# A branch moved to the kernel's end, layer 0's update around the last gathered rows, and layer 1's end bank by bank

## The chip, the core and the metric

The kernel runs on one core of a Trainium2 chip. A core has several engines that each work through a queue of their own: TensorE (PE, with its weight loads listed as PEld), VectorE (DVE), ScalarE (ACT), GpSimd (POOL) and SyncE (SP), which here only starts transfers. They wait for each other through semaphores. Sixteen DMA engines move the data. The metric is the device time of one execution in microseconds; lower is better.

## The reference

Four graph layers run one after another on the same 2708 nodes with 128 features each (`x`) and one 2708 by 2708 matrix `adj`, about 2.4% of which is not zero. After each layer stands a residual normalization.

```python
x = layernorm(x + layer0(x, adj))   # likewise layers 1, 2, 3

def layer0(x, adj):                 # a message for every edge
    s, d = x @ msg_w[:, :D].T, x @ msg_w[:, D:].T
    messages = gelu(s[:, None, :] + d[None, :, :] + msg_b)
    aggregated = einsum('ijd,ij->id', messages, adj)
    new = concatenate([x, aggregated], -1) @ upd_w.T + upd_b
    h = gelu(new) + x
    return normalize(h) * ln_w + ln_b

def layer1(x, adj):                 # gates for every pair
    m = x @ W_msg + b_msg
    gates = sigmoid((m @ W_q) @ (m @ W_k).T / sqrt(128) + gate_bias)
    aggregated = (gates * adj * adj) @ m
    h = relu(concatenate([x, aggregated], 1) @ W_upd + b_upd)
    return normalize(h) * gamma + beta
```

Layers 2 (hyperbolic attention) and 3 (two graph convolutions with swish) keep their code in this change; only where they stand in the program changes.

## The kernel before

The 2708 rows lie in 22 tiles of up to 128 partitions (`NT`; the last has 20 rows). Work that ends in a bank of PSUM (512 floats per partition) goes by `groups()`: five groups of four tiles, then tile 20 alone, then tile 21 with its 20 rows. The normalizations go by `runs()`, two halves of eleven tiles.

**Layer 0** never forms all pairs. It takes 22 row tiles of 125 rows against 22 blocks of 124 columns, picks up to five edges per row and block with one-hot products on PE (L716, L721), applies Gelu on ACT (L760), weighs on DVE (L747) and adds up on PE (L732). The rows' remaining, "far" edges, up to 16, are gathered one by one: `start_far` (SP) lays the row's own part from a table in DRAM, `s_tab`, into a buffer `far`, eight indirect transfers on POOL add the other end's part to it (L680), ACT applies Gelu (L686), DVE sums up with the edges' weights (`far_sum`, L692 and L694), and `turn` and `close` (PE L700 to L703, ACT L706) put the row tile's result into `aggT`. All of this is ordered by hand: every row tile yields steps with the number of the block at which each is due (`when`), and the loop over 484 blocks runs the steps that are due. Steps that are due beyond the last block remain; for the last row tile these are the second Gelu, eight far sums, `turn` and `close`.

Behind the loop a counter is made: `bad_n` (L777 to L785) is the number of rows with more far edges than there is room for, or with values that aren't finite. Then the remaining steps run. Then `new`, x's half of the update, which an earlier stage has stored in the table `u_tab`, is loaded (L791), `bad_n` is read into a register on every engine, and a branch (L793, L794) leads to a second way that goes through all pairs. With these inputs it is not taken. Then the update: POOL makes `xb`, x plus `ln_b` (L846); per group PE multiplies `aggT` with `upd_a` (L851), DVE adds `new` (L852), ACT applies Gelu (L853), DVE adds x (L854) and takes the statistics (`bn_stats`, L173). `resnorm` then normalizes by halves: a chain of some fifteen small DVE operations with one square root on ACT (the table of functions is loaded for it, L121), the normalization of the eleven tiles, two of three on DVE (L194) and the third on ACT (L192), times `ln_w` (L201), plus `xb` (L202), statistics again, and a second normalization into x. From the branch on, the order on each engine is not written by hand; the framework's scheduler lays groups and halves into each other.

**Layer 1** begins by multiplying the two gate weights into one (L880 to L885), turns x on PE (xT, L892, L893), forms the messages twice, turned (`mT`, L895, L896) and by rows (`mrow`, `sums` at L231 and L233), and `qT` (L898, L899); POOL makes `xb` (L901). Then 22 rows of tiles follow: six products into two buffers of PSUM (`lg`, L922), the sigmoid on ACT (L923) into a gate buffer `w` (two of them), two multiplications by the row of adj on DVE (L925, L926), and six products with `mrow` that add up in six banks of PSUM over all 22 rows (`acc`, L928). Then six copies to `aggT` (L930), the update (`sums` of x's and of the aggregate's half, Relu at L942), and `resnorm`. Small values of layer 2's weights are made beside this (`Weights2`: vectors by POOL's queue, L264, and a chain from L270 on).

SP's queue is in program order: the far rows, `new`, three of layer 1's rows of adj (`at`, L911), four of layer 2's (L1122), then each further row as buffers come free; at the end the `out` transfers.

Of the kernel before, what the change touches and what calls it, by code (L numbers as in the profile page):

```python
# [11 lines left out]
F32 = mybir.dt.float32  # L12
# [26 lines left out]
def gnn_stack(ctx: ExitStack, tc: tile.TileContext, t, out: bass.AP):  # L39
# [13 lines left out]

    def weight(name, k0=0):
        w = const.tile([P, D], F32, name=f"w_{name}_{k0}")
        nc.sync.dma_start(out=w, in_=t[name][k0:k0 + P, :])
        return w

    def column(name):
        c = const.tile([P, 1], F32, name=f"col_{name}")  # L60
        nc.sync.dma_start(out=c, in_=t[name].rearrange("(p o) -> p o", o=1))
        return c

    def across(name):
# [8 lines left out]
    nc.vector.memset(x[:, NT - 1, :], 0.0)  # L73
    if NFULL:
        nc.sync.dma_start(out=x[:, :NFULL, :], in_=t["x"][:NFULL * P, :].rearrange("(n p) d -> p n d", p=P))
    if NFULL < NT:
        nc.sync.dma_start(out=x[:rows[-1], NT - 1, :], in_=t["x"][NFULL * P:, :])
# [14 lines left out]
    class Values:  # L92
# [5 lines left out]
        def new(self, like=None):  # L98
            self.n += 1
            shape = [P, NT] if like is None else list(like.shape)  # L100
            return self.pool.tile(shape, F32, name=f"{self.tag}{self.n}")

# [93 lines left out]
    def resnorm(h, xb, g, st, V, sq=None):  # L196

        st2 = V.pool.tile([P, NT, 6], F32, name=f"{V.tag}_st2")
        for a, b in runs():
            normalize(h, h, st, a, b, V)  # L200
            nc.vector.tensor_tensor(h[:, a:b, :], h[:, a:b, :], over_tiles(g, b - a), op=ALU.mult)  # L201
            nc.vector.tensor_tensor(x[:, a:b, :], xb[:, a:b, :], h[:, a:b, :], op=ALU.add)  # L202
            moments(st2, x, a, b)
        for a, b in runs():
            normalize(x, x, st2, a, b, V, sq)
# [119 lines left out]
    with ExitStack() as l0:  # L325
# [6 lines left out]
        bad_n = wp.tile([1, 1], mybir.dt.int32, name="bad_n")  # L332
# [4 lines left out]
        with ExitStack() as msg:  # L337
# [167 lines left out]
            class Rows:  # L505
# [125 lines left out]
                def past(self, m):  # L631
                    if m == 0:
                        self.o = op_.tile([P, NB, JB], F32, name="o")
# [105 lines left out]

            LAG = 3  # L740
            assert NC == 5 and NB % 2 == 0
            R = [Rows(i) for i in range(LT)]
            steps = sorted(((g, n, step) for n, (g, step) in enumerate(x for v in [preparation(), *(v.when() for v in R)] for x in v)),
                           key=lambda x: x[:2])
            with tc.manual_schedule():
# [27 lines left out]

                most = vp.tile([P, 1], F32, name="most")
# [12 lines left out]
                for _, _, step in steps:  # L787
                    step()

        new = l0.enter_context(tc.tile_pool(name="l0x", bufs=1, reuse_waits="tile")).tile([P, NT, D], F32, name="new")  # L790
        nc.sync.dma_start(out=new, in_=u_tab.rearrange("(n p) d -> p n d", p=P))  # L791

        n_bad = nc.values_load(bad_n[0:1, 0:1])  # L793
        with tc.If(n_bad > 0), ExitStack() as msg:  # L794
            mp = msg.enter_context(tc.tile_pool(name="all", bufs=1))
            ap_ = msg.enter_context(tc.tile_pool(name="adjrows", bufs=2))
            gp = msg.enter_context(tc.tile_pool(name="gelu", bufs=3))
            psum = msg.enter_context(tc.tile_pool(name="ps_l0", bufs=2, space=PSUM))
            pbc = msg.enter_context(tc.tile_pool(name="ps_bc", bufs=2, space=PSUM))
# [3 lines left out]
            sel = mp.tile([3 * RG, RG], BF16, name="sel")  # L803
            nc.vector.tensor_add(sel, ident[:3 * RG, 0:RG], ident[:3 * RG, RG:2 * RG])
            nc.vector.tensor_add(sel, sel, ident[:3 * RG, 2 * RG:3 * RG])

            xT = mp.tile([P, N], F32, name="xT")
            sT = mp.tile([P, N], F32, name="sT")
            dT = mp.tile([P, N], F32, name="dT")
            transposed(xT, x, psum)  # L810
            linear_T(sT, msg_s, xT, psum, bias=msg_b)
            linear_T(dT, msg_d, xT, psum)

            HALF_N = -(-N // 2)
            halves = spans(0, N, HALF_N)
            part = mp.tile([P, N, len(halves)], F32, name="part")
            for g0 in range(0, N, RG):
                r0 = min(g0, N - RG)
                a = ap_.tile([3 * RG, N], F32, name="a")
                for k in range(3):  # L820
                    nc.sync.dma_start(out=a[k * RG:(k + 1) * RG, :], in_=adj[r0:r0 + RG, :])
                s = ap_.tile([3 * RG, N], BF16, name="s")
                nc.gpsimd.tensor_copy(s, a)
                for n in (2 * RG, RG):
                    nc.gpsimd.tensor_tensor(a[:n, :], a[:n, :], s[:n, :], op=ALU.subtract)
                    nc.gpsimd.tensor_copy(s[:n, :], a[:n, :])
                for i in range(g0, min(g0 + RG, N)):
                    one = sel[:, i - r0:i - r0 + 1].to_broadcast([3 * RG, P])
                    g = gp.tile([P, N], F32, name="g")
                    nc.scalar.activation(g, dT, AF.Gelu, bias=sT[:, i:i + 1])  # L830
# [124 lines left out]
    with ExitStack() as l2:  # L955
# [27 lines left out]
        with ExitStack() as pre:  # L983
# [9 lines left out]
            for k in range(2):  # L993
                nc.gpsimd.memset(prod[k], 1.0)
# [527 lines left out]
```

## Time and profile before

The median of three executions is 2005.69 us (2005.01 to 2007.13). The execution that the profiler took had 2005.42 us, of which 2003.7 are its span, first to last instruction; 1.7 us lie around it.

| stage | from, us | to, us |
|---|---|---|
| layer 0, preparation and block loop | 0 | 894 |
| layer 0, last far rows, branch | 894 | 914 |
| layer 0, update and normalizations | 914 | 954 |
| layer 1, ahead of its row loop | 954 | 988 |
| layer 1, row loop | 988 | 1214 |
| layer 1, update and normalizations | 1214 | 1257 |
| layer 2 | 1257 | 1765 |
| layer 3 | 1765 | 2004 |

Over the whole span PE is busy for 1675.0 us (84%), DVE for 1517.8 (76%), ACT for 1105.9 (55%) and POOL for 666.0 (33%). The mean clock granted to PE is 0.918 of full speed.

A line of the timeline has the start in us, the duration in us, the engine, the line of the kernel, the operation, what it writes and reads with shapes, and how many lie in the group; in brackets, how long the engine stood idle before it, and what it waited for. "q" behind an engine's name is its instruction queue. In the table of windows "PEclk" is the share of full clock that PE was granted, and the last two columns are the DMA engines' mean share and their throughput.

### The profile page before, as it was taken

The numbers are of one execution on the slowest core, as the hardware profiler recorded it, in microseconds if no ns is written. First come the engines' busy times: TensorE is split into PE (matmuls) and PEld (weight loads), VectorE is DVE, ScalarE is ACT, GpSimd is POOL, SyncE is SP. The second block draws the span as 40 slices with busy tenths as digits, with TensorE's granted clock in tenths as the row PEclk, the third lists the DMA queues.
The fourth block names the chain that finished last, engine by engine and source line by source line (L and its number), as shares of the span: only waits on it lengthen the run. The fifth ranks groups of instructions, "written<-read, shape, count | busy, mean of one in ns | idle before, by whom it ended". The sixth has DMA issues, their size and how long they took to land. (4 is left out here: it accounts for less than half of the span.)

```text
span 2003.7 us, 36396 instructions
## 1 busy us (share of the span) xinstructions
PE 1675.0 (84%) x14037; PEld 959.1 (48%) x14037; DVE 1517.8 (76%) x3507; ACT 1105.9 (55%) x1510; POOL 666.0 (33%) x417
## 2 busy tenths in 40 slices
PE   5799999999999999871899994689999974079996
PEld 5566666666666666651444433423222322034543
DVE  5899999999999999857556567889999997820105
ACT  3567667666666676642333331599998993300103
POOL 2467767757767667461100000012000350000000
PEclk8899999999999999995899996779998987579998
DMA  7666666666667666343133310022222215135230
GB/s 178 155 139 131 133 136 140 126 136 148 124 133 148 130 129 139 73 85 143 36 135 136 142 60 0 1 87 87 75 80 94 80 42 245 46 115 187 107 127 28
DMA packets 218358, 222.25 MB, mean 111 GB/s; under 512 B 28372, under 2 KB 204474, under 8 KB 211714
## 3 DMA queue, kind: packets, MB, share of 16 engines
q1 hardware_dynamic: 167038, 195.95, 32.2%
q0 software_dynamic: 51136, 23.88, 10.3%
q8 instruction: 112, 1.84, 0.4%
q14 instruction: 72, 0.59, 0.1%
HBM read 211.94 MB, written 7.83 MB: 110 GB/s over the span
## 5 line engine op out<-in xcount | busy, mean ns | idle before, releaser
L680 POOL DMA_INDIRECT far<-d_tab,ix x352 | 563.0, 1599 | 257.5 <-DVE W L747 110.7
L760 ACT ACTIVATE g<-sl 128x768 f32<-128x768 f32 x484 | 393.0, 812 | 255.9 <-PE sl L721 199.1
L716 PE MATMUL sl<-dA,S 124*128 124x153 f16 x4840 | 408.0, 231 | 10.1 <-DVE W L747 7.7
L716 PEld LDWEIGHTS <-S 124*128 124x128 f16 x4840 | 330.4, 98 | 79.7 <-issue 67.9
L732 PE MATMUL acc<-g,W 128*32 128x128 f32 x4840 | 205.5, 277 | 0.7 <-DVE ones L777 0.7
L1125 POOL TENSOR_TENSOR at<-at,off 128x128 f32<-128x128 f32 (+1 forms) x22 | 68.1, 3113 | 338.1 <-DMA at<-in_adjT 320.4
L1441 PE MATMUL acc<-held,x 128*128 128x512 f32 (+1 forms) x240 | 99.6, 563 | 84.0 <-DVE x L194 84.0
L732 PEld LDWEIGHTS acc<-g,W 128*32 128x32 f32 x4840 | 140.6, 109 | 58.9 <-issue 54.7
L721 PE MATMUL sl<-s,same 50*128 50x384 f16 x968 | 161.9, 308 | 0.0
L233 DVE TENSOR_TENSOR g<-ps,row_L_gnn_b 128x512 f32<-128x512 f32 (+2 forms) x14 | 7.9, 572 | 197.1 <-PE ps L231 197.0
L923 ACT ACTIVATE w<-lg,row_L_gnn_gate_bias 128x512 f32<-128x512 f32 (+1 forms) x132 | 80.7, 634 | 137.8 <-PE lg L922 74.3
L1181 PE MATMUL accV<-m,X 128*128 128x512 f32 (+4 forms) x264 | 128.4, 628 | 33.6 <-DVE m L1171 29.2
L747 DVE TENSOR_TENSOR W<-sl,own 128x150 f32<-128x150 f32 x484 | 143.0, 299 | 14.6 <-ACT g L760 14.1
L1133 PE MATMUL ps<-XT 128*128 128x512 f32 (+4 forms) x264 | 143.2, 626 | 3.1 <-ACT m L1138 2.8
L676 DVE FIND_INDEX8 ix<-v,o 128x8 uint32<-128x2728 f32 x44 | 131.7, 2993 | 0.0
L607 DVE TENSOR_SCALAR S<-rk 124x1000 f16<-124x1000 bf16 (+1 forms) x330 | 129.4, 418 | 0.0
L922 PE MATMUL lg<-qT,mT 128*128 128x512 f32 (+2 forms) x264 | 115.5, 567 | 13.5 <-ACT w L923 9.9
L925 DVE TENSOR_TENSOR w<-w,at 128x2708 f32<-128x2708 f32 (+1 forms) x22 | 65.4, 2974 | 79.3 <-ACT w L923 79.3
L694 DVE SCALAR_TENSOR_TENSOR extra<-far,v,extra 128x128 f32<-128x128 f32 x330 | 114.4, 347 | 12.3 <-ACT far L686 6.0
L1441 PE MATMUL acc<-at,x 128*128 128x512 f32 (+3 forms) x288 | 116.7, 552 | 0.0
L638 DVE SCALAR_TENSOR_TENSOR o<-ps,ar 128x496 f32<-128x496 f32 x132 | 82.4, 624 | 38.3 <-issue 22.6
L1400 ACT COPY nT<-acc 128x512 f32<-128x512 f32 (+1 forms) x12 | 6.4, 530 | 186.7 <-PE acc L1441 186.7
(310 smaller groups left out, 2687.1 us busy)
## 6 DMA issues: line engine op xcount, KB each, us to landing
at<-in_adjT SPq DMA_DIRECT2D x40, 1354.0 KB
ar<-in_adj SPq DMA_DIRECT2D x105, 248.0 KB
far<-s_tab SPq DMA_DIRECT2D x44, 512.0 KB
at<-in_adjT SPq DMA_DIRECT2D x42, 448.0 KB
at<-in_adjT SPq DMA_DIRECT2D x21, 704.0 KB
at<-in_adjT SPq DMA_DIRECT2D x21, 650.0 KB
held<-in_adjT SPq DMA_DIRECT2D x10, 1354.0 KB
at<-in_adjT SPq DMA_DIRECT2D x21, 280.0 KB
```

The lines of the kernel that those rows point to most:

```text
L607: nc.vector.tensor_scalar(self.S[h][:, :n, :, k * RG:(k + 1) * RG], self.rk[h][:, :n, :LR].rearrange("p b (c i) -> p b c i", c=NC), EDGE + ...
L676: nc.vector.max_index(ix, self.v[:, n * 8:n * 8 + 8], self.o.rearrange("p b j -> p (b j)"))
L680: nc.gpsimd.indirect_dma_start(out=self.far[n][:, k, :], out_offset=None, in_=d_tab[:, :], in_offset=bass.IndirectOffsetOnAxis(ap=self.ix[ ...
L716: nc.tensor.matmul(group[c], self.S[h][:, n, c, :], dA[q][:, b, c, :], start=c % 3 == 0 and q == 0, stop=False)
L721: nc.tensor.matmul(out, same[p], self.s3[p, :e - a, :], start=False, stop=True)
L732: nc.tensor.matmul(self.acc[q:q + 32, k, :], W[:, c, :], g[:, c, :], start=b == 0 and k == 0, stop=ends)
L747: nc.vector.tensor_tensor(W[:, :, :RG].rearrange("p (k c) i -> p k c i", k=2), columns_of(sl, D, DA), own[:, None, None, :].to_broadcast([ ...
L760: nc.scalar.activation(g.rearrange("p (k c) d -> p k c d", k=2), columns_of(sl, 0, D), AF.Gelu, scale=1.0 / D_SCALE)
L922: nc.tensor.matmul(lg[:r, :b - a], mT[:, j * P:j * P + r], qT[:, a:b], start=True, stop=True)
L1133: nc.tensor.matmul(ps, XT[:, self.js], XT[:, c], start=True, stop=False)
L1181: nc.tensor.matmul(accV[:, a:b], X[:self.r, self.j, :], self.m[:, a:b], start=first, stop=last)
L1441: nc.tensor.matmul(acc[k], src[:rows[j], j, :], at[:rows[j], a:b], start=j == order[0], stop=j == order[-1])
```

## The change

It has three parts.

The branch: everything from layer 1 on becomes a function, `layers_1_to_3`. It runs once, and only then is `bad_n` read and the branch taken or not; inside of it x is loaded anew, layer 0 is done through all pairs, and layers 1 to 3 are done again. The loads of weights are cached, so that the second pass finds the first one's.

Layer 0's update: a class `Update` loads `new` during the block loop (due at block 469 of 484) into a buffer of the pool of rows `o`, and its groups are written by hand around the last row tile's remaining steps: the five groups that don't need the last row tile come first, with the last Gelu after the second and the eight far sums after the third. Then `turn` and `close`, the first half's normalization, the two last groups, and the rest. x plus `ln_b` is made in place on POOL, group by group. The counter `bad_n` comes last. Statistics and small values lie in two buffers `g` of the block loop (`Values.within`).

Layer 1: the products of x with `W_msg` and with x's half of `W_upd` become one, 256 wide, into `both` (two tiles per bank, one addition of the joint bias). There are four gate buffers instead of two; the accumulator is six tiles. The last three rows' products are held back and done bank by bank by hand: three products, the copy to `aggT` (on ACT instead of DVE), and the update of the bank before, which adds only the aggregate's half; the first half's normalization stands after the fourth bank. Ahead of the row loop, the stage takes all eight banks of PSUM.

```diff
+    class Resnorm:
...
+        def add(self, a, b):
+            h = self.h
+            normalize(h, h, self.st, a, b, self.V)
+            nc.vector.tensor_tensor(h[:, a:b, :], h[:, a:b, :], over_tiles(self.g, b - a), op=ALU.mult)
+            nc.vector.tensor_tensor(x[:, a:b, :], self.xb[:, a:b, :], h[:, a:b, :], op=ALU.add)
+            moments(self.st2, x, a, b)
+
+        def end(self, a, b):
+            normalize(x, x, self.st2, a, b, self.V, self.sq)
...
+            class Update:
+                def when(self):
+                    yield (LT - 1) * NB + 7, self.load
+
+                def load(self):
+                    o = op_.tile([P, max(NB * JB, NT * D)], F32, name="o")
+                    self.new = o[:, :NT * D].rearrange("p (n d) -> p n d", d=D)
+                    nc.sync.dma_start(out=self.new, in_=u_tab.rearrange("(n p) d -> p n d", p=P))
...
+                def sums(self, n):
+                    a, b, r = groups()[n]
+                    g, ps = self.new[:r, a:b, :], sl_all[n % 3][:r, n // 3 % 2, :].rearrange("p (i d) -> p i d", d=D)
+                    for i in range(a, b):
+                        nc.tensor.matmul(ps[:, i - a, :], aggT[:, i * P:i * P + r], upd_a, start=True, stop=True)
+                    nc.vector.tensor_tensor(g, g, ps[:, :b - a, :], op=ALU.add)
+                    nc.scalar.activation(g, g, AF.Gelu)
+
+                def rows(self, n):
+                    a, b, r = groups()[n]
+                    g = self.new[:r, a:b, :]
+                    nc.vector.tensor_tensor(g, g, x[:r, a:b, :], op=ALU.add)
+                    moments(self.st, self.new, a, b)
+                    nc.gpsimd.tensor_tensor(x[:r, a:b, :], x[:r, a:b, :], over_tiles(ln_b, b - a, r), op=ALU.add)
...
+                U.open()
+                for n in range(ahead):
+                    U.sums(n)
+                    if n > 0:
+                        U.rows(n - 1)
+                    if n == 1:
+                        last_gelu()
+                    if n == 2:
+                        for step in far_sums:
+                            step()
+                for step in last_turn:
+                    step()
+                U.rows(ahead - 1)
+                early, late = runs()
+                U.norm.add(*early)
+                for n in range(ahead, G):
+                    U.sums(n)
+                for n in range(ahead, G):
+                    U.rows(n)
+                U.norm.add(*late)
+                U.norm.end(*early)
+                U.norm.end(*late)
...
-                for _, _, step in steps:
-                    step()
-
-        new = l0.enter_context(tc.tile_pool(name="l0x", bufs=1, reuse_waits="tile")).tile([P, NT, D], F32, name="new")
-        nc.sync.dma_start(out=new, in_=u_tab.rearrange("(n p) d -> p n d", p=P))
-        n_bad = nc.values_load(bad_n[0:1, 0:1])
-        with tc.If(n_bad > 0), ExitStack() as msg:
...
+            both = wp.tile([P, NT, 2 * D], F32, name="both")
+            mrow, h = both[:, :, :D], both[:, :, D:]
...
-                sums(mrow[:r, a:b, :], a, b, r, [(xT, w_msg)], psum, msg_br)
+                    for i in range(a, b, 2):
+                        m = min(i + 2, b)
+                        ps = psum.tile([P, 2, 2 * D], F32, name="ps_w")
+                        for k in range(i, m):
+                            nc.tensor.matmul(ps[:r, k - i, :], xT[:, k * P:k * P + r], w_both, start=True, stop=True)
+                        nc.vector.tensor_tensor(both[:r, i:m, :], ps[:r, :m - i, :], over_tiles(b_both, m - i, r),
+                                                op=ALU.add)
...
-            gp = att.enter_context(tc.tile_pool(name="gates", bufs=2))
+                LAST = 3
+                gp = att.enter_context(tc.tile_pool(name="gates", bufs=LAST + 1))
...
+                def update(k):
+                    per = BANK // D
+                    for a, b, r in groups():
+                        if k * per <= a < (k + 1) * per:
+                            ps = plog.tile([P, BANK], F32, name="lg")[:r].rearrange("p (i d) -> p i d", d=D)
+                            for i in range(a, b):
+                                nc.tensor.matmul(ps[:, i - a, :], aggT[:, i * P:i * P + r], upd_a, start=True, stop=True)
+                            g = h[:r, a:b, :]
+                            nc.vector.tensor_tensor(g, g, ps[:, :b - a, :], op=ALU.add)
+                            nc.scalar.activation(g, g, AF.Relu)
+                            moments(st, h, a, b)
...
+                    if j < NT - LAST:
+                        for k in range(len(banks)):
+                            add_up(j, k, w)
+                    else:
+                        kept_w.append((j, w))
+                with tc.manual_schedule():
+                    early, late = runs()
+                    for k, (a, b) in enumerate(banks):
+                        for j, w in kept_w:
+                            add_up(j, k, w)
+                        nc.scalar.copy(aggT[:, a:b], acc[k])
+                        if k > 0:
+                            update(k - 1)
+                        if (k - 1) * BANK < early[1] * P <= k * BANK:
+                            norm.add(*early)
+                    update(len(banks) - 1)
+                    norm.add(*late)
+                    norm.end(*early)
+                    norm.end(*late)
...
+    with ExitStack() as top:
+        layers_1_to_3(top)
+
+    n_bad = nc.values_load(bad_n[0:1, 0:1])
+    with tc.If(n_bad > 0), ExitStack() as top:
+        load_x()
+        all_pairs()
+        layers_1_to_3(top)
```

## The prediction, made before the changed kernel ran

> **What bounds the kernel now.** I read the two stretches that the change rewrites, from layer 0's last row tile to layer 1's start (894 to 988 us) and layer 1's loop end to layer 2 (1200 to 1264), first as busy time by stage (columns: window, its length, busy us and instructions of PE, PEld, DVE, ACT, POOL, then granted clock, DMA share, GB/s).
>
> ```profile
> 894.00:908.00 14.00, 2.27 (x12) 1.64 (x8) 3.86 (x14) 1.94 (x6) 0.22 (x1) 0.63 0.43 113
> 908.00:914.00 6.00, 0.47 (x3) 0.76 (x4) 0.00 (x0) 0.00 (x0) 3.25 (x1) 0.50 0.37 117
> 914.00:954.00 40.00, 7.61 (x45) 6.80 (x44) 35.27 (x146) 11.50 (x26) 3.02 (x2) 0.59 0.39 160
> 954.00:970.00 16.00, 11.53 (x30) 6.88 (x31) 3.77 (x13) 4.21 (x7) 7.64 (x4) 0.63 0.16 13
> 970.00:988.00 18.00, 17.46 (x81) 10.65 (x81) 8.46 (x22) 8.03 (x17) 0.00 (x0) 1.00 0.00 1
> 988.00:1200.00 212.00, 200.14 (x495) 83.43 (x493) 124.00 (x44) 77.14 (x127) 0.00 (x0) 1.00 0.33 119
> ```
>
> For 20 us (894 to 914) nothing is busy for more than 4 us; then DVE is the bound (35 of 40), then PE at half clock, then PE at full clock, which holds the whole row loop. The timeline says what the first 20 us wait for, and how the loop ends:
>
> ```profile
> 892.13 0.71 SPq L791 DMA_DIRECT2D new<-u_tab  x1
> 901.37 1.06 ACT L686 ACTIVATE far<-far 128x1024 f32<-128x1024 f32 x1 [6.52 <-issue]
> 902.46 3.06 DVE L694 SCALAR_TENSOR_TENSOR extra<-far,v,extra 128x128 f32<-128x128 f32 x8 [6.02 <-ACT far L686]
> 907.50 0.26 ACT L706 COPY aggT<-ps 128x125 f32<-128x125 f32 x1 [5.08 <-PE ps L703]
> 913.53 7.39 PE L851 MATMUL ps<-w_L_upd_wT,aggT 128*128 128x128 f32 x44 [6.06 <-issue]
> 915.49 0.69 DVE L852 TENSOR_TENSOR new<-new,ps 128x512 f32<-128x512 f32 x1 [9.97 <-PE ps L851]
> ...
> 1200.52 4.81 PE L928 MATMUL acc<-w,mrow 128*128 128x512 f32 x12 [1.40 <-DVE w L926]
> 1206.40 7.51 PE L928 MATMUL acc<-w,mrow 20*128 20x512 f32 x12 [1.07 <-DVE w L926]
> 1213.94 3.30 DVE L930 COPY aggT<-acc 128x512 f32<-128x512 f32 x6 [7.60 <-PE acc L928]
> 1217.22 0.17 DVE L938 MEMSET h<- 128x128 f32 x1
> ```
>
> The last gather was issued by 894.2, yet its Gelu starts at 901.4: the u_tab load, issued at 892.1, fills the DMA engines meanwhile (share 1.04 and 1.02 in 896 to 900, 0.31 just before). After close (907.8) the branch L794 holds every engine until 910.7 and the first usable product until 913.5. At the loop's end the two last products and six copies run in series, 1200.5 to 1217.2.
>
> **The Trainium skill.** "TensorE: Matmul & The Clock Gate", Part 1, has the clock double after about 3.4 us of sustained work and fall after an idle window. Layer 1's tail agrees (restart 1217.4, full 1221.8), its start doesn't: restart 954.4, full at 969.6, with a gap at 963 to 966. "SBUF — State Buffer", Who interferes with whom, has a DVE operation with two SBUF inputs contend with a GpSimd one that reads SBUF; the trace agrees: L1125 on POOL takes 0.44 alone and 2.8 in the mean beside layer 2's vector work. "ScalarE: Activation LUTs", What ACT_TABLE_LOAD costs, gives 1283 ns plus a drain of 1380; the trace shows 1.28 and no drain.
>
> **Part 1, layer 0's update.** Removed: the load's collision, the branch in the middle, and the wait of the update for the last row tile; groups 0 to 4 are done while its far rows land. Added or moved onto DVE's path: nothing but order. On DVE from 895.3 (PE's first four products, 0.9 after the last weigh): per group the add .61 and, a group later, +x .56 with bn_stats .87, so 1.43. s0 .61, s1 .61, r0 1.43, s2 .61, r1 1.43 gives 900.0; the far rows should be there by then, so the far sums' 3.06 give 903.1; s3, r2, s4, r3, r4 (.61+1.43+.61+1.43+1.43) 908.6. add(early): the small-operation chain 2.65 (what the same chain takes at layer 3's end, 1977.9 to 1980.6, where order is also by hand), table load 1.28 exposed, normalize 2.16, ×ln_w 1.55, +x 1.55, bn_stats 2.15, .3 of gaps: 920.2. Groups 5 and 6: 1.8, 922.0. add(late), its table load hidden: 10.1, 932.1. end(early) 4.8, end(late) 4.6: 941.5. POOL's x+=ln_b, now in seven pieces beside two-input vector work (before, one of 6.12), costs 0 to 3; I take .8: x done at 942.3, where before it was 953.5. Then the bad_n count (895.1 to 896.5 before, hidden) stands ahead of layer 1 with w_q's transposes: 1.56 exposed. Layer 1's x transposes start at 945.4 against 954.8: −9.4. SP's order: the u_tab load now stands behind one far<-s_tab and ahead of the second, at about 868; that one, issued at 854.6 before, lands about 880.5 where its gathers want it at 879.7. 0 to 2 us, and hidden, since DVE reaches the far sums only at 900.0.
>
> **Part 2, layer 1's start.** Before, 954.8 to the first gate product at 988.3: 33.5. After: x's half of the update rides in 256-wide products, +.2 per tile of 22 on PE. The gap of 963 to 966 is DVE's L270, waiting until 965.0 for y_vecs, whose DMAs POOL issues only after xb (953.9 to 960.0); now POOL's xb begins when x is done, 3.1 ahead of PE's transposes, and at most 1 us of the gap is left. With the clock full 5 us after the start, as in layer 1's tail, qT is done 29.5 after, 974.9. PSUM is full now (four names by two buffers), so row 0's logits follow instead of lying between: 5.3, plus sigmoid's table load 1.28 and .5 of latency: 982.0. So −6.3 in all; 3.1 of the 9.4 go back. If PE stays at half clock as before, less: bounds −2 to −11.
>
> **Part 3, layer 1's loop.** Before, 988.3 to the last gates at 1206.4: 218.1. PE is full (200 of 212): 24 product records 9.48 and 12 logits pairs 10.94 per two rows. After, rows 19 to 21's products but one bank stand behind row 21's logits: .83 of a row's 4.74, −3.9. Four gate buffers let logits run ahead where PE waited for DVE (2.5) or ACT (9.9 in all): 0 to −4, I take −2. DVE is busy 124 of 212, but its last three rows then come in series, +.6. Last gates at 1194.8, −11.6.
>
> **Part 4, layer 1's tail.** Before, 1206.4 to layer 2's first scalar chain, 1263.3: 57.0. Now, per bank, three products at .86 and the update's .9 at .21 to .25 each, cold at first after some 5 us of waiting; ACT's copy .55; the moments of group 2 at +15.8, add(early) 10 after that (26), groups 3 to 6 at add .69, Relu .63, bn_stats .87 in series, 2.2 for the full two and .94 for the small two (32.4), add(late) 9.8, end(early) 6.5 with layer 2's memset and xsq, end(late) 5.9: +54.4, and 5.3 on to layer 2 (before, 6.1 from 1257.3; the late half's copies alone stand behind x now): 59.7. So +2.8: the pieces removed (6.6 of products and 3.3 of copies in series, half of the update's products) are paid back by DVE's hand-written order, which waits for ACT where the order of before filled the holes. Bounds −3 to +6.
>
> **Part 5, the branch at the end.** Its middle cost (907.8 to 913.5, 5.8) is in part 1. At the end each engine loads bad_n, compares and joins; L794's rows say from branch to join 5.1 on SP, 4.3 POOL, 2.9 DVE, 3.8 PE, 2.6 ACT.
>
> ```profile
> L794 SPq COMPARE_BRANCH  x1: 54/54/54, 897.0 to 897.0; - x1
> L794 PEldq COMPARE_BRANCH  x1: 3766/3766/3766, 906.2 to 906.2; - x1
> L794 ACTq COMPARE_BRANCH  x1: 50/50/50, 908.0 to 908.0; - x1
> ```
>
> SP issues its last out transfer at 2000.3 and would join about 2006; the span ends at 2003.7 for the transfers' sake. So +3, bounds +.5 to +6. SP's queue: layer 2's first at loads, issued at 914 before, now stand behind layer 1's 22 and wait for its buffers, to about 1240; four of 704 KB take some 16 us, wanted at about 1285: hidden, and up to +5 if not. Layers 2 and 3: 0.
>
> **Sum.** Layer 1 begins 9.4 earlier; its start gives 3.1 back (−6.3), its loop takes 5.3 (−11.6), its tail gives 2.8 back: −8.8 at layer 2. The branch at the end, +3: −5.8 on the profiled 2005.42, which stands .27 under the median of 2005.69. Forecast 1999.5 (1999.6 rounded); its own range is 1994.5 to 2002, from parts 3 and 5 alone at their ends.
>
> **Rivals.**
> R1, more gain: PE is warm within the first 5 us and row 0 follows closely (−4 more in part 2), the four buffers give their whole 4 (−2 more), and the branch hides behind the out transfers (+.5 for +3): −14.3, 1991. For: each removed wait is plain in the trace. Against: three parts have to come out at their good ends, and chains ordered by hand leave holes on DVE.
> R2, no change: POOL's additions take the 3 us (+2.2), the end costs 6 (+3): −.6, 2004.8; the late far rows or the tail at its worst give about the same. For: L1125's nineteen microseconds for its longest show how far POOL can fall behind DVE. Against: all of x+=ln_b is wanted only from 909 on, long after its issue.
> R3, slower, one mechanism: PE stays at half clock through layer 1's start, because the many small products keep waiting for ACT's and DVE's copies out of PSUM. The start holds 23 us of work counted at full clock (17.5 in 970 to 988, half of the 11.5 before) and now 4.4 more (.2 × 22); I have 2.5 of it doubled. With 12 more doubled: −5.8+12, 2011.6. It decides once more than 10 us (5.8 and the bound of 4) run at half clock beyond what I have. For: before, the clock was low through the first 15 us. Against: that stretch had its gap of 3 us, which goes.
>
> **How the numbers follow.** Forecast .47, R1 .23, R2 .20, R3 .10. A measurement of this kernel can't tell .2%, 4 us, from no change. Faster (under 2001.7): R1 and nearly all of the forecast's cases, .68. Same: most of R2, .21. Slower: R3 and a rest of R2, .11. The range takes in R1 with 2 us of its own spread and R2 with as much, and leaves R3 out: 1989 to 2007.
>
> **What would show it.** Part 1: x's last normalization at 942, no idle of 6 us on DVE ahead of the far sums. Part 2: first gate product near 982, clock 1.0 by 952. Part 3: last gates at 1195. Part 4: 57 to 60 us from there to layer 2. Part 5: last engine joins 3 us after the transfers. Wrong if the late far rows reach DVE's path, if layer 2's first rows wait for their at loads, or if the clock stays low.

## The result, and the profile after

The changed kernel takes 2010.91 us (median of 20 executions, 2004.5 to 2015.22) where the kernel before takes 2006.59 (median of 20, 2004.9 to 2008.41). The ratio is 1.0023, with a 95% interval of 1.0017 to 1.0029: slower by 0.2%, 4.3 us, where 5.8 us of gain were forecast. It also varies more: its executions lie 10.7 us apart, those of before 3.5.

The profiled execution took 2013.94 us, 3.0 above its kernel's median; its span is 2012.2, 8.5 more than before. The loop over layer 0's blocks, which the change doesn't touch, began its last weighing Gelu 2.8 us later in it (894.9 against 892.1; in the other runs of this study that point lies between 891.7 and 895.9). So the stages are compared from that point on. A gate product is DVE's product of a row's gates with its row of adj; the table has the start of the first and the end of the last, the "last gates". Layer 2's scalar chain is the run of small operations that DVE begins there. All values are us after the last weighing Gelu:

| until | before | after | forecast gain | measured gain |
|---|---|---|---|---|
| x of layer 0 is done | 61.4 | 51.9 | 11.2 | 9.5 |
| first gate product of layer 1 | 96.2 | 95.4 | 6.3 | 0.8 |
| last gate product's end | 314.2 | 304.8 | 11.6 | 9.4 |
| layer 2's scalar chain | 371.2 | 370.7 | 8.8 | 0.5 |
| DVE's last instruction | 1107.9 | 1108.4 | 8.8 | −0.5 |
| the span's end | 1111.6 | 1117.3 | 5.8 | −5.7 |

Every stage's gain comes and is given back in the stage after it. Layer 0's update gains 9.5, layer 1's start loses 8.7 of them; the row loop gains 8.6, the tail loses 8.9; the end loses 5.2. The table of windows of the changed kernel (columns as before):

```profile
894.00:914.00 20.00, 10.37 (x101) 8.39 (x98) 15.74 (x45) 5.79 (x12) 9.68 (x8) 0.81 0.09 11
914.00:954.00 40.00, 5.49 (x17) 3.68 (x18) 30.04 (x120) 12.33 (x26) 7.00 (x8) 0.50 0.13 47
954.00:988.00 34.00, 26.99 (x92) 16.00 (x90) 15.20 (x37) 10.87 (x19) 2.92 (x4) 0.95 0.20 73
988.00:1194.70 206.70, 196.72 (x492) 83.00 (x491) 125.31 (x45) 79.69 (x130) 0.00 (x0) 1.00 0.34 122
1194.70:1214.00 19.30, 14.55 (x23) 5.54 (x22) 6.58 (x7) 1.80 (x3) 0.00 (x0) 0.56 0.00 1
1214.00:1222.00 8.00, 8.00 (x29) 3.73 (x28) 3.46 (x13) 3.71 (x5) 0.00 (x0) 1.00 0.00 0
```

The empty 20 us of before (894 to 914) are filled: DVE works 15.7 of them instead of 3.9. But from 914 to 954 DVE, the bound of that stage, is busy for only 30.0 of 40, and PE for 5.5. The timeline of layer 1's start shows what that stage then waits for:

```profile
947.89 1.30 SPq L1046 DMA_DIRECT2D at<-in_adjT  x3
947.89 0.31 POOL L975 MEMSET both<- 128x256 f32 x1 [20.61 <-DVE most L880]
948.32 0.47 PE L983 MATMUL ps<-ident,w_L_gnn_W_q 128*128 128x128 f32 x1 [0.24 <-DVE bad_n L883]
949.11 6.14 POOL L1010 TENSOR_TENSOR xb<-x,row_L_gnn_ln_beta 128x2816 f32<-128x2816 f32 x1
956.36 0.55 POOL L299 DMA_DIRECT2D y_vecs<-in_L_gnn_att_wr  x1
958.29 1.12 PE L1001 MATMUL ps_q<-mT,w_qk 128*128 128x512 f32 x2
963.12 0.56 DVE L305 TENSOR_TENSOR y_prods<-y_vecs 128x384 f32<-128x384 f32 x1 [6.60 <-DMA y_vecs<-in_L_gnn_att_wr]
964.34 2.02 PE L1007 MATMUL ps_w<-w_both,xT 128*128 128x256 f32 x4 [4.92 <-DVE both L1008]
```

Two lines of the kernel before, for comparison:

```profile
910.73 3.01 SPq L911 DMA_DIRECT2D at<-in_adjT  x3
965.02 0.56 DVE L270 TENSOR_TENSOR y_prods<-y_vecs 128x384 f32<-128x384 f32 x1 [3.76 <-DMA y_vecs<-in_L_gnn_att_wr]
```

x is done at 946.8, but layer 1's first operations on POOL and PE (L975, L983) wait for the count of bad_n, which stands last in layer 0's order by hand; so POOL begins xb only at 949.1. SP could issue layer 1's first rows of adj only at 947.9, when layer 0's buffers were free (before: 910.7). POOL finished xb at 955.3 and issued the last of y_vecs at 956.4, into 4 MB of rows that were under way. DVE had taken up the operation on y_vecs (L305) and waited 6.6 us for it; behind it stood the additions that empty PE's banks, so PE stood still for 4.9 us.

At layer 1's end, the timeline of PE:

```profile
1193.92 1.13 PE L1029 MATMUL acc<-w,both 128*128 128x512 f32 x2 [1.14 <-DVE w L1061]
1199.80 7.78 PE L1029 MATMUL acc<-w,both 20*128 20x512 f32 x8 [4.75 <-DVE w L1061]
1207.52 2.08 PE L1037 MATMUL lg<-w_L_gnn_W_upd,aggT 128*128 128x128 f32 x8
1209.38 4.99 PE L1029 MATMUL acc<-w,both 128*128 128x512 f32 x6
1214.30 1.16 PE L1037 MATMUL lg<-w_L_gnn_W_upd,aggT 128*128 128x128 f32 x8
1215.29 2.93 PE L1029 MATMUL acc<-w,both 128*128 128x512 f32 x6
```

PE waits 4.75 us for row 21's gates, and the clock falls to half (0.56 in the mean from 1194.7 to 1214). Six records of a product then take 4.99 us, and 2.93 after 1214, when the clock is back. It had worked without a gap from 1199.8 to 1213.6 by then.

The end: SP's last line in the timeline of the changed kernel, and then the rows of the branch (line, queue, instruction, its durations in ns, first and last start in us):

```profile
2003.53 0.99 SPq L1610 DMA_DIRECT2D out<-x  x1
```

```profile
L1635 SPq EVENT_SEMAPHORE  x8: 17/17/17, 2008.0 to 2010.5; - x8
L1635 PEldq COMPARE_BRANCH  x1: 3695/3695/3695, 1989.6 to 1989.6; - x1
L1635 SPq COMPARE_BRANCH  x1: 54/54/54, 2005.3 to 2005.3; - x1
L1635 DVEq EVENT_SEMAPHORE  x1: 21/21/21, 2006.1 to 2006.1; - x1
```

SP issues the last transfer, reads bad_n, branches at 2005.3 and is past the join at 2010.5; every other engine is there by 2006.1. From DVE's last instruction to the span's end it takes 8.9 us, before 3.7.

### The profile page after: what moved, and what is told of

The parts are those of the page before. It is cut to its first block, busy times and chain, and to the rows that moved or that the text cites. A ratio compares the mean times of both kernels' runs of the same rounds, so it can differ in the third digit from the quotient of the medians.

```text
span 2012.2 us, 36316 instructions
## 1 busy us (share of the span) xinstructions
PE 1675.8 (83%) x13993; PEld 953.7 (47%) x13993; DVE 1530.5 (76%) x3505; ACT 1114.6 (55%) x1519; POOL 670.1 (33%) x428
## 3 DMA queue, kind: packets, MB, share of 16 engines
q0 software_dynamic: 51136, 23.88, 10.1%
## 5 line engine op out<-in xcount | busy, mean ns | idle before, releaser
L751 PE MATMUL sl<-dA,S 124*128 124x153 f16 x4840 | 408.3, 232 | 10.5 <-DVE W L816 8.0
L816 DVE TENSOR_TENSOR W<-sl,own 128x150 f32<-128x150 f32 x484 | 143.3, 300 | 14.1 <-ACT g L829 13.5
L1317 PE MATMUL accV<-m,X 128*128 128x512 f32 (+4 forms) x264 | 123.9, 610 | 35.3 <-DVE m L1307 33.3
L1029 PE MATMUL acc<-w,both 128*128 128x512 f32 (+2 forms) x264 | 111.3, 568 | 5.9 <-DVE w L1061 5.9
```

What stands on the lines that cost most here:

```text
L751: nc.tensor.matmul(group[c], self.S[h][:, n, c, :], dA[q][:, b, c, :], start=c % 3 == 0 and q == 0, stop=False)
L816: nc.vector.tensor_tensor(W[:, :, :RG].rearrange("p (k c) i -> p k c i", k=2), columns_of(sl, D, DA), own[:, None, None, :].to_broadcast([ ...
L1317: nc.tensor.matmul(accV[:, a:b], X[:self.r, self.j, :], self.m[:, a:b], start=first, stop=last)
```

## The experiments

Every kernel was timed in five rounds beside the kernel before. Ratios are to the kernel before, with 95% intervals; the changed kernel itself stands at 1.0023. "After the Gelu" means us after the last weighing Gelu, as in the table above.

| | median, us (executions) | ratio | interval |
|---|---|---|---|
| e1, no branch | 2007.0 (13) | 1.0002 | 0.9994 to 1.0011 |
| e2, branch behind layer 0 | 2009.91 (21) | 1.0021 | 1.0015 to 1.0028 |
| e3, vectors loaded first | 2007.59 (21) | 1.0008 | 1.0001 to 1.0016 |
| e4, PE kept busy | 2005.9 (13) | 0.9999 | 0.9991 to 1.0007 |
| e5, layer 1's tail not by hand | 1996.04 (6) | 0.9957 | 0.9943 to 0.997 |
| e6, vectors used late | 2004.69 (21) | 0.999 | 0.9984 to 0.9997 |
| e7, layer 1 as before | 2008.26 (13) | 1.0007 | 0.9999 to 1.0015 |
| e8, three amendments | 1996.54 (5) | 0.9949 | 0.9937 to 0.9962 |
| e9, e5 with two amendments | 1985.45 (4) | 0.9894 | 0.9879 to 0.9909 |
| e10, PE's order alone | 2003.1 (21) | 0.9988 | 0.9981 to 0.9995 |
| e11, e9, layer 0's end not by hand | 1970.36 (5) | 0.9825 | 0.9812 to 0.9838 |
| e12, both ends not by hand | 1984.7 (4) | 0.9889 | 0.9872 to 0.9905 |

### The branch: e1 and e2

```diff
-    n_bad = nc.values_load(bad_n[0:1, 0:1])
-    with tc.If(n_bad > 0), ExitStack() as top:
-        load_x()
-        all_pairs()
-        layers_1_to_3(top)
```

> Leaves out the reading of bad_n, the branch and the second way behind it, at the kernel's end; the rest is the changed kernel. My theory (the branch at the end is paid in full, since SP meets it last: from DVE's last instruction to the span's end 8.9 us in the changed kernel, 3.7 in the one before): 5 us less than the changed kernel, about 2006, the same as before within 1 us. Rival (the transfers of out hide most of it, as I priced it with 3 or less): 2 to 3 us less, about 2008.5.

3.9 us less by the medians, between the two accounts, and 3.8 us instead of 8.9 from DVE's last instruction to the span's end in its profile. The profile shows that little of the branch at the end is hidden; the medians alone don't separate 5 from 3.

```diff
+    n_bad = nc.values_load(bad_n[0:1, 0:1])
+    with tc.If(n_bad > 0):
+        load_x()
+        all_pairs()
     with ExitStack() as top:
         layers_1_to_3(top)
```

> The changed kernel with the branch directly behind layer 0's update, around all_pairs alone; layers 1 to 3 follow once. My theory: at that place it costs what it did before the change, 5 to 6 us, and the 5.2 at the end go: within 1.5 us of the changed kernel, about 2011. Rival (a branch costs less where engines reach it one after the other and only SP's way through it is long): 3 to 5 us faster than the changed kernel, about 2007.

1.0 us less than the changed kernel, within my bounds. The first gate product comes 6.3 us later after the Gelu (101.7), the end is 5.1 shorter. In the profiles the branch costs five to six us at either place, by the medians 2.9 in the middle (e2 over e1) and 3.9 at the end: what part 1 of the forecast booked as a gain in the middle comes back at the end.

### Layer 1's start: e3 and e6

```diff
+            weights2 = Weights2(wp)
+            weights2.load()
+
             with ExitStack() as pre:
...
-                    if j == NT // 4:
-                        weights2.load()
-                    elif j == NT // 2:
+                    if j == NT // 2:
```

> The changed kernel with the loads of layer 2's small vectors (y_vecs, y_cols) written ahead of layer 1's first stage, so that POOL issues them before xb and SP ahead of the rows of adj. My theory (DVE's first operation on y_vecs waits 6.6 us for them, since they are issued behind xb and land behind 4 MB of rows of adj, and PE stands still 5 us for it): PE has no gap of over 1 us in layer 1's start, first gate product 4 to 5 us sooner after x is done, 2006.5. Rival (PE's half clock and the products of ahead of the rows set this stage, the gap only fills time): 0 to 2 us less, 2010.

My account was half wrong. The loads were issued 8 us sooner, but then took longer: 8.6 us from the issue of the last one to DVE's start, where the changed kernel has 6.2. The timeline of e3_vecs_first:

```profile
947.67 0.56 POOL L299 DMA_DIRECT2D y_vecs<-in_L_gnn_att_wr  x1
956.80 0.56 DVE L305 TENSOR_TENSOR y_prods<-y_vecs 128x384 f32<-128x384 f32 x1 [8.21 <-DMA y_vecs<-in_L_gnn_att_wr]
959.23 3.55 PE L1010 MATMUL ps_w<-w_both,xT 128*128 128x256 f32 x8 [3.68 <-DVE both L1011]
```

The first gate product came only 1.2 us sooner after the Gelu. The scheduler had put DVE's operation further ahead as well, and it waited longer. The transfers share the DMA engines with the rows of adj, and to be issued first helped little. By the medians e3 is 3.3 us faster than the changed kernel, again between the two accounts. This stage doesn't explain that: of the 4.9 us that e3's profile gains up to DVE's last instruction, 1.2 lie here, 1.2 in layer 1's tail, whose clock is back sooner, and 2.5 in layers 2 and 3, whose code is the same. What remains is to let nothing wait for them:

```diff
                         weights2.turn(plog.tile([P, BANK], F32, name="lg"))
+                        weights2.prods = gp.tile([P, N], F32, name="w")[:, :3 * D].rearrange("p (k d) -> p k d", d=D)
                         weights2.bias_point()
```

> The changed kernel with the products of layer 2's small vectors (L305) written into a gate buffer of layer 1's row 11, so that DVE can't take them up ahead of the rows, while the vectors are on their way. My theory (DVE's wait for y_vecs stops PE for 5 us in layer 1's start; to load them sooner didn't help since they land behind 4 MB of rows of adj either way): no gap of over 1 us on PE between 950 and 983, first gate product 90 us after the last weighing Gelu instead of 95.4, 4 to 5 us less, 2006.5. Rival (the stage's length is set by ACT's copies and the products): gap gone, first gate product at +94 and more, 2010.

L305 now runs at 1074, in the tenth row, and PE has no gap of over 0.6 us in layer 1's start up to the first row's own products. The first gate product comes 88.9 us after the Gelu, 6.5 sooner where I expected 5.4, and the medians say 6.2. The wait was the stage's loss, and it was more than PE's idle time of 4.9 us: in the changed kernel the clock falls to 0.50 for another 3.4 us behind it, here it stays at 1.00.

### Layer 1's tail: e4, e5 and e10

```diff
                         for j, w in kept_w:
+                            if k == 0 and j == NT - 1:
+                                idle = plog.tile([P, BANK], F32, name="lg")
+                                for i in range(6):
+                                    nc.tensor.matmul(idle, mT[:, i * P:(i + 1) * P], qT[:, :BANK], start=True, stop=True)
                             add_up(j, k, w)
```

> The changed kernel with six additional products, 128 by 512, whose result nobody reads, on PE between the first bank's second and third held product, where PE stands 4.75 us idle. My theory (the idle time drops PE to half clock, and the banks then take 5.3 us each instead of 3.5 until the clock is back 12 us later): the statistics of group 2 are done 16 us after the last gates instead of 22, 5 to 6 us less in all, 2005.5. Rival (DVE sets the tail, and PE's clock in it is hidden): 0 to 1 us less, 2010.5.

5.0 us less; group 2's statistics are done 15.6 us after the last gates instead of 21.9. The table of windows of e4_warm:

```profile
1192.00:1198.00 6.00, 5.30 (x13) 2.43 (x14) 5.97 (x3) 0.29 (x2) 0.00 (x0) 1.00 0.00 0
1198.00:1204.00 6.00, 6.00 (x20) 2.49 (x19) 0.53 (x1) 1.17 (x2) 0.00 (x0) 1.00 0.01 3
1204.00:1210.00 6.00, 6.00 (x20) 2.65 (x20) 2.88 (x10) 1.85 (x3) 0.00 (x0) 1.00 0.00 0
```

More work on PE made the kernel faster, because the clock stayed at 1.00. From the last gates to layer 2 it takes 59.4 us instead of 65.8; the forecast was 59.7. So the clock is as large as the whole error of part 4.

e5_free_tail takes away only the line `with tc.manual_schedule():` ahead of the tail.

> The changed kernel with layer 1's last products, copies, update and normalizations left to the scheduler's order instead of being written by hand; the operations are the same. My theory of the prediction (DVE's order by hand waits for ACT where the scheduler's order fills the holes, some 3 us): 2 to 4 us less than the changed kernel, 2008. Rival (the tail is long because PE runs at half clock, which no order of DVE's changes): within 1.5 us of it, 2011.

Both were too small: 14.9 us less. From the last gates to layer 2 it takes 45.5 us, against 65.8 in the changed kernel and 57.0 before. In its timeline PE works on the held products of rows 19 and 20 while it would wait for row 21:

```profile
1192.73 9.90 PE L1029 MATMUL acc<-w,both 128*128 128x512 f32 x22
1201.81 0.58 ACT L1071 COPY aggT<-acc 128x512 f32<-128x512 f32 x1 [8.28 <-PE acc L1029]
```

The statistics of groups 0 to 2 are complete 10.5 us after the last gates. How much of it is PE's order, and how much DVE's, tells e10, which keeps all orders by hand but PE's:

```diff
-                    for k, (a, b) in enumerate(banks):
-                        for j, w in kept_w:
-                            add_up(j, k, w)
+                    for k in range(len(banks)):
+                        for j, w in kept_w[:-1]:
+                            add_up(j, k, w)
+                    for k, (a, b) in enumerate(banks):
+                        add_up(*kept_w[-1][:1], k, kept_w[-1][1])
                         nc.scalar.copy(aggT[:, a:b], acc[k])
```

> The changed kernel, its tail still by hand, but with PE's order in it changed: the held products of rows 19 and 20 for all six banks first, then row 21's bank by bank with the copies and updates as they were. DVE's and ACT's orders are the changed kernel's. My theory (of the 20 us that the scheduler's order saved from the last gates to layer 2, one half is PE's: it works in the time in which it waited for row 21's gates, and stays at full clock): group 2's statistics 12 us after the last gates, 9 to 10 us less, 2001. Rival (DVE's order by hand makes up most of it): 4 to 6 us less, no more than e4_warm, 2005.5.

Group 2's statistics are done 12.3 us after the last gates, and layer 2's scalar chain begins 56.2 after them: 9.6 of the 20.3 us between e5 and the changed kernel are PE's order with its clock. The other 10.7 are what else the scheduler's order changes, on DVE and ACT above all; that is a difference, and no run changed DVE's order alone. By the medians PE's part is 7.8, between the two accounts.

### Layer 1 as before, and the combination: e7, e8 and e9

e7_l1_before puts the whole text of layer 1 from the kernel before into the changed kernel.

> Layer 1 as before the change (two gate buffers, mrow alone ahead of the rows, x's half in the update, the tail ordered by the scheduler), with the new layer 0 update and the branch at the end. My theory: layer 0's update is worth 9.5 us up to x, of which layer 1's start keeps 5 (its wait for y_vecs takes the rest), the loop and tail are those of before, and the end costs 5.2: the same as before within 2 us, 2006, so layer 1's part of the change costs 4 to 5. Rival (layer 1's part of the change is worth what its loop gains, 8.6 us): 2015.

1.8 us more than the kernel before: within the bounds. The new layer 0 update with the branch at the end doesn't pay by itself, since only 4.0 of its 9.5 us reach the first gate product (92.2 after the Gelu). Layer 1's part of the change costs what is left to the changed kernel, 2.6 us by the medians, where I expected 4 to 5: its gain in the row loop is real, and its start and tail take more.

e8_three joins e4's and e6's edits, and hands the last transfers to ACT:

```diff
+                q = nc.scalar if b == NT else nc.sync
                 if a < m:
-                    nc.sync.dma_start(out=out[a * P:m * P, :].rearrange("(n p) d -> p n d", p=P), in_=x[:, a:m, :])
+                    q.dma_start(out=out[a * P:m * P, :].rearrange("(n p) d -> p n d", p=P), in_=x[:, a:m, :])
```

> The changed kernel with three amendments: the vectors' products late as in e6_y_late, the six products that keep PE warm as in e4_warm, and the last two transfers of out issued by ACT instead of SP, so that SP is past the branch before the end. My theory (three separate losses of 4, 5 and 3 us): 1999, faster than before by 0.3%. Rival (they overlap, or SP's way through the branch isn't what ends last): 2003 to 2005.

14.4 us less than the changed kernel. SP takes its branch at 1981.2, before the end, and the span ends 5.6 us after DVE's last instruction instead of 8.9. The three losses add: measured one by one they were 5.0 (e4), 6.2 (e6) and 3.3 (this end), 14.5 in all, where I had put them at 12.

e9_free_three is e5 with e6's edit and these transfers.

> The changed kernel with layer 1's tail left to the scheduler (e5_free_tail), the vectors' products late (e6_y_late) and the last transfers of out issued by ACT (as in e8_three). My theory (three losses in three places, which add): 15 and 6 and 3 us less than the changed kernel, 1987. Rival (the scheduler had already used the time that the wait for y_vecs took elsewhere): 1992.

25.5 us less than the changed kernel, the sum of 15, 6 and 3 and 1.5 more.

### Layer 0's end: e11 and e12

e11_l0_free moves the lines from `U.rows(ahead - 1)` to the copy into bad_n out of the block that is ordered by hand; e12_free_both has that and e5's edit alone.

> e9_free_three with the end of layer 0's update, from the fifth group's statistics on, and the count of bad_n left to the scheduler as well. My theory (an order by hand leaves DVE idle in each chain of small operations): x is done 46 us after the last weighing Gelu instead of 51.9, 5 us less than e9_free_three. Rival (the order of layer 0's tail is bound by DVE's work itself, 46.7 us of it from 898 on in the changed kernel): 0 to 2 us less.

15.1 us less than e9_free_three, three times what I expected, and by another way. x is done 51.1 us after the Gelu, hardly sooner than by hand (51.9). What moves is layer 1. The timeline of e11_l0_free:

```profile
909.75 1.31 SPq L1046 DMA_DIRECT2D at<-in_adjT  x3
932.02 0.45 PE L995 MATMUL ps<-ident,x 128*128 128x128 f32 x1 [13.93 <-DVE x L218]
938.59 1.91 PE L1007 MATMUL ps_w<-w_both,xT 128*128 128x256 f32 x4
945.09 1.88 DVE L218 TENSOR_SCALAR x<-x,g 128x128 f32<-128x128 f32 x7
```

PE begins to turn x at 932, as soon as its first tile is normalized, and is through two groups by the time that DVE finishes x. The first gate product comes 74.8 us after the Gelu, 14.1 before e9's. Layer 1's loads, too, are issued sooner, 13.8 us after the Gelu instead of 53.0.

Why layer 1 could not begin beside the order by hand is shown only in part. An order by hand does not in itself keep out what follows: in the changed kernel's tail of layer 1, also by hand, PE begins to turn x for layer 2 at 1252.5, 7.5 us before x is done at 1260.1. At layer 0's end the lines above show layer 1's first operations waiting for the count of bad_n, which by hand stands last (946.7 to 948.3). The scheduler begins the count at 898.7 and ends it at 916.1, and layer 1's first product again follows it at once:

```profile
916.17 0.47 PE L983 MATMUL ps<-ident,w_L_gnn_W_q 128*128 128x128 f32 x1 [3.57 <-DVE bad_n L883]
```

e11 and e12 free both, the order of the normalizations and the place of the count. To move the count alone to where the kernel before had it, ahead of the update, would tell them apart; this was not tried.

> The changed kernel with nothing altered but the two orders by hand at the ends of layers 0 and 1, which are left to the scheduler (as in e11_l0_free, without its late products of the vectors and its transfers by ACT). My theory (the two orders by hand are what the change loses by; e11_l0_free was 15 us faster than e9_free_three since layer 1's start begins on PE beside layer 0's second half): 15 and 15 us less than the changed kernel, 1981, and y_vecs' wait partly covered now, so as low as 1977. Rival (it needs the late vectors, else DVE's wait for them stops layer 1's start as before): 1990 or more.

26.2 us less, between the two accounts. Without the late vectors their chain comes into layer 0's end, where DVE waits 6.0 us for y_vecs: x is done 59.5 us after the Gelu instead of 51.1, the first gate product at 85.0. Still, giving up the two orders by hand alone turns the loss of 4.3 us into a gain of 21.3 over the kernel before; with all amendments (e11) it is 35.7, 1.75%, the fastest kernel of the study.

## Why the prediction was wrong

The forecast was a gain of 5.8 us, the medians show a loss of 4.3. The steps below are measured in the two profiled executions, where the loss is 5.7 (counted from the Gelu).

**Part 1, layer 0's update** held up to the end of x. The gather no longer collides with the u_tab load: its last rows land 2.7 us after POOL has issued them (898.0 to 900.7), before it was 7.1. The far sums begin at 903.2 (forecast 900.0, in a loop that ended 2.8 sooner), and x is done 1.7 us later than the sum said, relative to the loop. The term for POOL's additions, .8, isn't there: the full ones take 1.26 to 1.28 each and nobody waits for them. (The mean of 2.8 us for L1125 that the prediction names hides two kinds: of the 18 beside layer 2's work ten took 0.45 to 0.52 us, and six 7.6 to 19.0.) What it left out is that nothing of layer 1 begins beside it; in the kernel before nothing did either (PE turned x from 954.8 on, x was done at 953.5), so it was no part of the forecast, but e11 shows 14 us there.

**Part 2, layer 1's start**, failed at "at most 1 us of the gap is left". I had found the gap's cause, DVE's wait for y_vecs, and reckoned that POOL would now issue them in time, since its xb would begin when x is done, 3.1 us ahead of PE's transposes. It began 0.9 ahead of them (949.1 and 950.0; before, 1.1), because the count of bad_n holds up POOL as well as PE. Then the transfer took longer: 6.2 us from the end of the last issue to DVE's start, before 3.4. The rows of adj, issued at 910.7 before, could be issued only at 947.9, and the vectors landed with the last of them: a transfer that used to be out of the way was moved beside another. The prediction asked of every moved step which queue it goes past, but I followed only layer 2's loads through SP, not layer 1's. The stage took 43.5 us from x to the first gate product, where the forecast's terms make 39.7 (before, 34.8). With the wait gone (e6) it takes 37.0, so the other terms were 2.7 too high, and the error of 3.8 is less than the wait's 6.5.

**Part 3, the loop**, gained 8.6 instead of 5.3 (from the first gate product to the last 209.4 us; 218.0 before, and again in e7). Whether the four buffers or the held products gave the 3.3 more was not tried.

**Part 4, the tail**, failed at the clock, "cold at first after some 5 us of waiting". The wait came as forecast, 4.75 us; but where part 2 had counted on full clock 5 us after a restart, "as in layer 1's tail", PE worked for 13.8 us at half clock, and the term of +2.8 was 6.1 too small. The Trainium skill, "TensorE: Matmul & The Clock Gate", Part 1, has the clock return after about 3.4 us of sustained work; the tail of before seemed to agree with 4.4, and I took that. Here it took 13.8. Nor was the 4.4 a clean case: in the tail of before the clock had already fallen at 1208.3, under row 21's products, and stayed at 0.50 for 13.7 us, of which the restart was only the last part. e4, whose clock never falls there, takes 59.4 for the forecast's 59.7; since the forecast held some half clock of its own, that the rest comes out so closely is in part luck. (The pieces of the sum as written make 54.6 and not 54.4; nothing hangs on it.) What I read as a small loss by DVE's order, 2.8 over the order of before, was in truth about half of 20 us that the scheduler's order of the same operations is worth (e5, e10).

**Part 5, the branch**, was sized at 3 within .5 to 6, and costs 5.2 in the profile and 3.9 by the medians (e1). SP's own 5.1 us from branch to join stood in the prediction. The step that was too short is SP's way from the start of its last issue to the join: I had 5.7 us (2000.3 to 2006), it took 7.0 (2003.5 to 2010.5), and the span ended 1.7 us behind the join, for which I had nothing.

The rival that ended slower had PE at half clock through layer 1's start. Its time, 2011.6, lies close to the 2010.9 measured, but that is luck: half clock was a right mechanism in the wrong stage. The start ran at .95 of full clock from 954 on, the tail at .56, and the tail is about half of the error. The forecast's errors by stage, in us: 1.7 in part 1, 3.8 in part 2, −3.3 in part 3, 6.1 in part 4, 2.2 in part 5, and 1.0 in layers 2 and 3, which is no more than their text, the same in all kernels, varies by (735.0 to 739.5 us from layer 2's chain to DVE's last instruction). They are the 11.5 between a gain of 5.8 and a loss of 5.7.

## What to carry to other kernels

Before an order is written by hand, ask what the scheduler does with the same operations, what behind the block could have begun inside it, and whether something that the next stage waits for stands last in it. This change's operations gained 1.1% with the scheduler's order (e12), and lost 0.2% with the one by hand. When a stage ends earlier, follow the loads that its end releases, and look for what they will now run beside. An engine that waits five microseconds for a short cause can pay for it in the work that follows, so fill such a wait with work that is held back anyway; and let the engine that issues the last transfers not be the one with the longest way to the end.

## What the runs showed of the hardware

The return to full clock isn't of a fixed length. In the same place of five kernels PE was idle for 4.75 us, its clock fell to 0.50, and PE then worked without a gap; the clock was back after 13.8 us of work (changed kernel), 13.6 (e1), 11.5 (e3), 10.6 (e2) and 6.4 (e6), and in the tail of the kernel before 4.6 us after PE's restart. The stretches at 0.50 themselves lasted 17.1, 17.1, 13.7, 13.7 and 10.2 us, before 13.7: all multiples of 3.4 us.

Work without a gap does not always hold the clock either. In e10 PE works from 1191.1 to 1210.5 without idle time, and at 1208.0 the clock falls all the same (PEclk 0.51):

```profile
1208.00:1210.50 2.50, 2.50 (x10) 1.95 (x10) 1.79 (x11) 1.76 (x3) 0.00 (x0) 0.51 0.00 0
```

In the tail of the kernel before it fell at 1208.3, with no gap of over 1.4 us in the 14 us before. In both places PE was at the products of row 21, which have 20 rows instead of 128 (in e10 with the update's between them); the slow returns above have such products between others too. Whether they are the reason was not tried.

The clock doesn't explain the spread of the times by itself. The changed kernel's executions lie 10.7 us apart and those of e9 and e12, whose PE doesn't fall idle at the last gates, 1.8 and 1.6 (four executions each); but e4, e5, e10 and e11, where it doesn't either, spread by 6.9, 10.1, 7.4 and 6.4 us. What makes the spread stays open.

A small transfer that shared the DMA engines with large ones gained little by being issued first: in e3 y_vecs, issued from 946.5 to 948.2, was there for DVE 8.6 us after the end of its last issue, with 4 MB of rows issued from 947.3 on. In the kernel before, with no rows under way, this took 3.4 us.
